# Small transformer: Silus of a result placed behind its last row, weighted sums of gathered rows with contiguous operands

## The chip, the cores and the metric

The kernel runs on one core of a Trainium2 chip. The metric is the device time of one execution in microseconds (us); three runs give its median. The profile is one further execution, whose own time is shown beside its span.

The engines are called as in the profile: PE (TensorE matmul; PEld is its weight load), DVE (VectorE), ACT (ScalarE), POOL (GpSimd) and SP (SyncE, which issues most transfers). PEclk is the TensorE clock that was granted, as a share of full speed.

## The reference

Four layers, each of them `x = x + attn(layernorm(x)) * silu(ffn(layernorm(x)))`, over 16 rows of 256 tokens with 128 features in float32. The change touches the end of layer 2 and layer 3.

Layer 2's feed-forward part is a mixture of 16 experts with two chosen for each token:

```python
topv, topi = jax.lax.top_k(probs, 2)
gate = jnp.sum(jax.nn.one_hot(topi, 16) * topv[..., None], axis=-2)
h = jax.nn.relu(jnp.einsum('bsd,edh->bseh', tensor, W1) + b1)
y = jnp.einsum('bseh,ehm->bsem', h, W2) + b2
out = jnp.einsum('bse,bsem->bsm', gate, y)
```

Layer 3 joins two parts that read the same normalized input:

```python
xn = _layernorm(x, axis=-1)
s = _L3_attn_ref(xn, ...)         # 16 heads of 8 features, with a penalty that depends on the distance
g = _silu(_L3_ffn_ref(xn, ...))   # two local transformer layers: attention in windows of 64, then a gated MLP
x = x + s * g
```

Each of the two local layers shifts half of the features by one token, projects to q, k and v with 8 heads of 64 features, attends within windows, adds the result to its input, and adds a gated MLP with an exact Gelu.

## The kernel before

Tokens lie on the 128 partitions, 32 tiles of 128 tokens. The arrays `x`, `xn`, `s` (the attention part) and `xnT` (the transposed input) stay in on-chip memory throughout.

**End of layer 2.** The experts wrote their results to DRAM, sorted by expert. For each tile `bring` (in `ffn2`) gathers the two chosen rows of each token with an indirect DMA from POOL's queue, and `weigh` adds both, times their gates, to the sum `f` (lines 1577 to 1582). `f` is a view of the memory of `xnT`, and the profile shows it under that name. The helper `mixed` (line 85) turns a row of 128 elements into a view of 64 x 2, so that elements are visited in the order 0, 64, 1, 65 and so on. Behind the sums, a Silu on ACT (line 937), a product with `s`, the sum into `x` and a layernorm give the input of layer 3. These pieces have names in the order list: `Ga` gathers a tile, `wa` weighs one, `su` is the Silu, `pw` the power of the layernorm.

**The local layers.** `local_layers` (called by `layer3`) works on blocks of 256 tokens; 16 blocks and two layers give 32 block numbers. Its work is cut into small pieces, one function each (decorator `@piece`). An order written out by hand, the string `LOCAL`, lists the pieces with a row number each; the loop "for turn in ..." runs through the list once for each turn, and a piece with row number r works on block turn + r. So a turn issues one block's worth of every piece, each at another stage of its block. ACT's pieces in a turn are copies of PSUM results (`hT`, `v`, `qT`, `kT`, `pT`, `oT`), squares (`sq`), 32 exponentials of the softmax (line 2033), and three Gelus (line 2177). Exponentials and Gelus need different function tables; a table load is an instruction of its own (ACT_TABLE_LOAD). The blocks' results are kept in place in `X`, which is the memory of `xn`; the last addition to a block is the piece `Z` (line 2205) of the second layer.

After the loop `pin(mark)` (line 988) binds every instruction since `mark` to the one ahead of it on the same engine, so that within the loop each engine issues in the order of the program text. Instructions outside of that are put in place by the framework's scheduler.

**The Silus.** Behind the call of `local_layers`, `layer3` issues eight Silus on ACT, each over four tiles of `X` (lines 1755 to 1757). They are outside of the pinned stretch, and the scheduler put seven of them between pieces of the second local layer, one in every second turn, and the eighth behind the last Gelu.

**The last attention.** `attn3` calls `attn8`. It projects q and k for two blocks at a time (`project`): a matmul into PSUM (line 292), an eviction with bias on ACT (line 299), a write to DRAM (`qkd`, line 301) and eight reads back in another layout (`qT`, `kT`, line 306), all on SP's queue. Then come the scores `pa` (line 345), their row maxima on DVE, the scores again, transposed (`pb`), the exponential, a product with the penalty, and the weighted values. The first two projections stand ahead of that function's own pinned loop. A later piece, `done`, multiplies `s` by `X` and adds it to `x`, and stores the result; it is the reader of the Silus.

Of the kernel before, what the change touches and what calls it, by code (L numbers as in the profile page):

```python
# [13 lines left out]
AF = mybir.ActivationFunctionType  # L14
ALU = mybir.AluOpType
# [8 lines left out]
NT = B * S // P  # L24
# [60 lines left out]
def mixed(*tiles):  # L85

    axes = {2: "p (a b) -> p b a", 3: "p t (a b) -> p t b a"}
    return [t.rearrange(axes[len(t.shape)], a=2) for t in tiles]


class Net:
# [20 lines left out]
    def load(self, pool, ap, name, shape=None, eng=None):  # L112
        t = pool.tile(list(shape or ap.shape), F32, name=name)
        (eng or self.nc.sync).dma_start(t, ap)
        return t
# [1201 lines left out]
    def ffn2(self, ctx, consts, f, keep):  # L1317
# [4 lines left out]
        nc, tc, a = self.nc, self.tc, self.a  # L1322
# [5 lines left out]
        wr, br, b1, step, row = consts  # L1328
        slot = keep.tile([P, K, NT], I32, name="slot", bufs=1)
        gate = keep.tile([P, K, NT], F32, name="gates", bufs=1)  # L1330
# [101 lines left out]
        placed, got = [], {}  # L1432
# [143 lines left out]

        def weigh(t):
            for k in range(K):
                y, row = mixed(f[:, t, :], got.pop(("rows", t, k)))
                nc.vector.scalar_tensor_tensor(  # L1580
                    y, row, gate[:, k, t : t + 1], y, ALU.mult, ALU.add
                )

        return {
            "send": send, "begin": begin, "piece": piece, "pieces": 4 * NB + 4, "bring": bring,
            "weigh": weigh, "spread": spread, "biases": biases, "biased": biased,
        }

# [149 lines left out]
    def layer3(self, end, out):  # L1738

        nc, tc = self.nc, self.tc
        X = self.xn
        right = lambda n, **kw: tc.tile_pool(name=n, bufs=1, side="right", **kw)
        with ExitStack() as ctx:
            gp = ctx.enter_context(right("a3_g"))
            dram = ctx.enter_context(tc.tile_pool(name="a3_d", bufs=1, space=DRAM))
            with right("f3_w") as cp:
                layers, load = self.local_weights(cp)
                with tc.tile_pool(name="l2_g", bufs=4) as got:  # L1750
                    gather = end["Ga"]
                    end["Ga"] = end["Gb"] = lambda: gather(got)
                    end["wb"] = end["wa"]
                    g, dr = self.local_layers(X, layers, load, end, lambda: self.gates3(gp, dram))
            for c in range(NT // 4):
                xc = X[:, 4 * c : 4 * c + 4, :]
                nc.scalar.activation(xc, xc, AF.Silu)

            def done(b, store):
                ts = slice(2 * b, 2 * b + 2)  # L1760
                if store:
                    nc.sync.dma_start(out[:, ts, :], self.x[:, ts, :])
                else:
                    attn, ffn = mixed(self.s[:, ts, :], X[:, ts, :])
                    nc.vector.tensor_mul(attn, attn, ffn)
                    nc.gpsimd.tensor_add(self.x[:, ts, :], self.x[:, ts, :], self.s[:, ts, :])

            self.attn3(g, dr, done)
# [83 lines left out]
        return r  # L1852

    def local_layers(self, X, layers, load, end, gates):

# [15 lines left out]
        nc, tc = self.nc, self.tc  # L1873
        with ExitStack() as ctx:
# [17 lines left out]
            rows = {b: {"l": layers[b // B], "X": X[:, 2 * (b % B) : 2 * (b % B) + 2, :]} for b in range(2 * B)}  # L1892
# [315 lines left out]
            gate, gates = gates()  # L2208
# [5 lines left out]
            for n in LOCAL.split():  # L2214
                n, row = n.split(":")
# [10 lines left out]
            for turn in range(-max(rows_), 2 * B - min(rows_)):  # L2226
                for n, args, row in order:
                    b = turn + row
                    if n in ("Ga", "Gb", "wa", "wb", "su", "pw"):
                        end[n]()  # L2230
                    elif n in ("gp", "ge", "gs", "gw", "gt", "gr"):
                        gate(n, b, psm)
                    elif 0 <= b < 2 * B:
                        do.get(n[0] + "_", do.get(n[0]))(b, *args)
                        w = spent.get(n + "".join(map(str, args)))
                        if b == B - 1 and w:
                            load(1, w)
            self.pin(mark)
            return gates

# [44 lines left out]
```

## Time and profile before

| | |
|---|---|
| median of 3 runs | 2729.04 us (2728.78 to 2735.28) |
| profiled execution | 2734.26 us, of which span 2732.5 us |
| mean granted TensorE clock | 0.918 |
| PE busy | 2346.4 us (86% of the span) |
| DVE busy | 1962.1 us (72%) |
| ACT busy | 1668.4 us (61%) |
| POOL busy | 1384.6 us (51%) |
| first and last weighted sum (line 1580, 64 of them) | 1435.8 and 1713.8 us |
| first and last table load for a Silu of line 1757 | 1994.7 and 2312.4 us |
| first score of the last attention (line 345) | 2322.4 us |

Times within the profile count from the start of the span. A line of the timeline gives start, duration, engine, line of the kernel, operation, output and inputs, and in brackets how long the engine had been idle and what ended that. A group's line gives busy time and mean duration, then the idle time ahead of the group. Instructions on ACT and DVE overlap by a little, so that the distance from start to start of two neighbours is up to 0.1 us shorter than the first one's duration. The busy share of an engine over the whole span says little about one stage, so stages are looked at in stretches of their own.

### The profile page before, as it was taken

How to read it: one execution, taken by the hardware profiler on the slowest of the kernel's cores; microseconds unless marked ns; L12 is line 12 of the kernel's file. 1: busy time of each engine (PE TensorE's matmuls, PEld its weight loads, DVE VectorE, ACT ScalarE, POOL GpSimd, SP SyncE). 2: the span in 40 equal slices, each digit the busy share in tenths (PEclk: the TensorE clock that was granted, in tenths of full speed). 3: DMA queues.
4: the chain of work that ended last, by engine and by line, in shares of the span. 5: the costliest groups of instructions: out<-in, count | busy, mean ns of one | idle time of the engine just before them, and what ended most of it. 6: DMA issues, size and time to landing. Idle time of an engine off the chain costs nothing.

```text
span 2732.5 us, 47736 instructions
## 1 busy us (share of the span) xinstructions
PE 2346.4 (86%) x17672; PEld 1560.2 (57%) x17735; DVE 1962.1 (72%) x3810; ACT 1668.4 (61%) x3680; POOL 1384.6 (51%) x1162
## 2 busy tenths in 40 slices
PE   6999997899756799999983789999999997889887
PEld 4666667566432455555561456666666665655554
DVE  6666633555579688888877899877776662788775
ACT  2555554233235466676641788888999896565653
POOL 3000001422417666666566667565654554798886
PEclk7999998899668899999996999999999998899987
DMA  3001002000114456556552000000000001121210
GB/s 84 24 29 33 17 17 101 6 11 12 35 54 152 142 165 196 180 182 189 173 185 57 21 22 23 15 19 18 24 11 11 13 14 32 33 46 30 49 30 9
DMA packets 136917, 168.25 MB, mean 62 GB/s; under 512 B 20850, under 2 KB 100604, under 8 KB 136684
## 3 DMA queue, kind: packets, MB, share of 16 engines
q1 hardware_dynamic: 128108, 147.09, 18.2%
q0 software_dynamic: 6496, 17.05, 1.8%
q8 instruction: 140, 2.29, 0.4%
q10 hardware_dynamic: 2080, 1.05, 0.1%
q14 instruction: 93, 0.76, 0.1%
HBM read 126.96 MB, written 29.79 MB: 57 GB/s over the span
## 4 chain that ended last, share of the span: by engine, by line
PE 27%; DVE 14%; ACT 11%; POOL 9%; issue 3%; DMA 2%; SPq 1%; POOLq 0%; DVEq 0%; ACTq 0%
PE py L1253 4%; ACT p L2033 3%; POOL e L333 3%; PE pm L2168 2%; PE pm L1922 2%; PE ps L2009 2%; PE ph L1496 2%; DVE pen L1715 2%; PE pa L1098 2%; PE pm L2096 1%; PE py L1519 1%; PE pb L355 1%; PE pa L345 1%; DVE sn L1948 1%; DVE ss L1944 1%
## 5 line engine op out<-in xcount | busy, mean ns | idle before, releaser
L366 DVE TENSOR_REDUCE nmax<-pa 128x2 f32<-128x512 f32 x512 | 329.6, 683 | 135.6 <-PE pb L355 109.1
L376 ACT ACTIVATE e<-pb 128x512 f32<-128x512 f32 x512 | 286.2, 594 | 226.8 <-PE pb L355 204.8
L355 PE MATMUL pb<-qa,kT 32*128 32x256 f32 x2048 | 388.4, 424 | 32.9 <-ACT e L376 32.9
L345 PE MATMUL pa<-kT,qT 32*128 32x256 f32 x2048 | 365.9, 435 | 10.9 <-DMA kT<-qkd 8.2
L1243 POOL TENSOR_TENSOR hc<-st,cn 128x1024 f32<-128x1024 f32 x111 | 261.2, 2353 | 193.7 <-DVE dbb L1226 120.9
L1230 DVE TENSOR_TENSOR_SCAN st<-dab,dbb 128x1024 f32<-128x1024 f32 x128 | 292.7, 2287 | 23.5 <-ACT dab L1216 8.1
L355 PEld LDWEIGHTS pb<-qa,kT 32*128 32x128 f32 x2048 | 249.8, 196 | 62.7 <-ACT e L376 54.0
L345 PEld LDWEIGHTS pa<-kT,qT 32*128 32x128 f32 x2048 | 231.4, 201 | 93.1 <-issue 56.2
L1253 PE MATMUL py<-hc,ident 128*128 128x512 f32 x512 | 270.6, 619 | 8.8 <-DVE hc L1243 7.4
L333 POOL TENSOR_TENSOR e<-e,pen 128x1024 f32<-128x1024 f32 x96 | 229.1, 2394 | 62.7 <-ACT e L376 61.5
L1922 PE MATMUL pm<-qkv,hT 128*128 128x512 f32 x384 | 211.9, 636 | 32.0 <-ACT p L2033 12.2
L2033 ACT ACTIVATE p<-ps,nm,rl 128x128 f32<-128x128 f32 x512 | 230.0, 474 | 12.2 <-DVE nm L2024 11.7
L1216 ACT ACTIVATE dab<-dl,A_log 128x512 f32<-128x512 f32 x256 | 177.7, 718 | 97.2 <-DVE st L1230 56.2
L178 POOL TENSOR_SCALAR ln_r<-ln_mv 128x4 f32<-128x4 f32 x32 | 8.5, 264 | 446.3 <-DVE ln_mv L189 438.6
L1957 POOL TENSOR_TENSOR rot<-rot,sn 128x512 f32<-128x512 f32 x128 | 162.6, 1274 | 125.7 <-DVE sn L1948 125.5
L1226 DVE TENSOR_TENSOR dbb<-du,bn 128x1024 f32<-128x1024 f32 x128 | 187.5, 1465 | 5.5 <-DMA bn<-dr 2.8
L2052 POOL TENSOR_TENSOR p<-p,den 128x512 f32<-128x512 f32 x128 | 130.5, 1041 | 39.7 <-DVE den L2047 30.7
L1253 PEld LDWEIGHTS py<-hc,ident 128*128 128x128 f32 x512 | 92.8, 197 | 80.7 <-issue 61.4
L1519 PEld LDWEIGHTS py<-w,h 128*128 128x128 f32 x752 | 101.1, 197 | 59.2 <-issue 39.7
L402 PE MATMUL pm<-e,vaug 128*32 128x256 f32 x2048 | 129.1, 394 | 3.6 <-DVE s L436 3.6
L1937 ACT ACTIVATE sq<-pm 128x512 f32<-128x512 f32 x128 | 76.4, 597 | 78.5 <-PE pm L1922 71.6
L1510 ACT ACTIVATE h<-ph,b1s 128x256 f32<-128x256 f32 x188 | 78.6, 470 | 70.0 <-PE ph L1496 69.1
(390 smaller groups left out, 5614.5 us busy)
## 6 DMA issues: line engine op xcount, KB each, us to landing
bn<-dr SPq DMA_DIRECT2D x64, 512.0 KB
cn<-dr SPq DMA_DIRECT2D x64, 512.0 KB
w<-in_L_ffn_W_dram SPq DMA_DIRECT2D x94, 256.0 KB
qkd<-qk SPq DMA_DIRECT2D x32, 256.0 KB
v<-v SPq DMA_DIRECT2D x64, 128.0 KB
f_y<-y SPq DMA_DIRECT2D x47, 128.0 KB
f_x<-zero POOLq DMA_DIRECT2D x8, 704.0 KB, 6.7
xr<-f_x SPq DMA_DIRECT2D x44, 128.0 KB
```

What stands on the lines that cost most here:

```text
L333: eng.tensor_mul(pairs[m], pairs[m], pen.to_broadcast([P, 2, 2, S]))
L345: nc.tensor.matmul(pa[:, t, :], qbuf[b % 4][r : r + 32, g, ts], kbuf[b % 4][r : r + 32, g, :], start=True, stop=True,)
L355: nc.tensor.matmul(pb[:, t, :], kbuf[b % 4][r : r + 32, g, ts], qas[m // 8][r : r + 32, g % 2, :], start=True, stop=True,)
L366: nc.vector.tensor_reduce(nbuf[n // 8 % 2][:, :, u // 4, u % 4, 8], pa, AX.X, ALU.max, negate=True)
L376: nc.scalar.activation(e, pb, AF.Exp, scale=scale)
L1216: nc.scalar.activation(d["da", r - r % 2][:, r % 2, :], d["dl"][:, h, :], AF.Exp, scale=an[:, h, n : n + 1])
L1226: mul = nc.vector.tensor_mul(db, du, d["bn", n])
L1230: nc.vector.tensor_tensor_scan(wide(d["st", r]), wide(d.pop(("da", r))), wide(db), 0.0, ALU.mult, ALU.add)
L1243: ins = eng.tensor_mul(d["hc", r], d.pop(("st", r)), d["cn", r // 4 * 2])
L1253: nc.tensor.matmul(d["py", h], self.ident, d["hc", r - r % 2][:, r % 2, :], start=(n == 0), stop=(n == N - 1))
L1922: nc.tensor.matmul(pj, hTs[b % 3][:, t * P : (t + 1) * P], rows[b]["l"]["qkv", j], start=True, stop=True,)
L2033: nc.scalar.activation(p[:, c, w, :], rows[b]["ps", u][i][:, c, w, :], AF.Exp, scale=rows[b]["r"][:, w, 0, h + 2 * c : h + 2 * c + 1], bia ...
```

## The change

Two edits. In `weigh`, the operands of the weighted sum are plain rows of 128 elements in place of the 64 x 2 views; operation, engine and number are the same. And the loop of eight Silus moves from `layer3` to the end of `local_layers`, between the loop over turns and `pin(mark)`, so that they are pinned on ACT behind the last piece.

```diff
@@ ffn2, weigh
             for k in range(K):
-                y, row = mixed(f[:, t, :], got.pop(("rows", t, k)))
                 nc.vector.scalar_tensor_tensor(
-                    y, row, gate[:, k, t : t + 1], y, ALU.mult, ALU.add
+                    f[:, t, :], got.pop(("rows", t, k)), gate[:, k, t : t + 1], f[:, t, :],
+                    ALU.mult, ALU.add,
                 )
@@ layer3
                     g, dr = self.local_layers(X, layers, load, end, lambda: self.gates3(gp, dram))
-            for c in range(NT // 4):
-                xc = X[:, 4 * c : 4 * c + 4, :]
-                nc.scalar.activation(xc, xc, AF.Silu)
-
             def done(b, store):
@@ local_layers, behind the loop over turns
                         if b == B - 1 and w:
                             load(1, w)
+            for c in range(NT // 4):
+                xc = X[:, 4 * c : 4 * c + 4, :]
+                nc.scalar.activation(xc, xc, AF.Silu)
             self.pin(mark)
             return gates
```

In the changed program's order of issue, ACT has eight Silus behind one table load after the last three Gelus and ahead of the eviction of the first q projection (in the kernel before: that eviction, a table load, one Silu, the eviction of k). SP issues both `qkd` writes, then the eight `qT` reads, then the eight `kT` reads; before, it issued the write and the reads of q, then the write and the reads of k. The order on PE, DVE and POOL is the same as before.

## The prediction

> **What bounds the kernel now.** The page's busy shares (PE 86%, DVE 72%, ACT 61%) average over stages with different limits, so I cut out the stages that the change touches: the windowed attention stage in front of layer 3 (1430 to 2314 us, one "turn" of the order list per 256 rows), and the seam behind it, where the last attention starts (2300 to 2325). First view: busy time in stretches, each from one Gelu table load on ACT to the next, so one turn each.
>
> ```profile
> core 0: us, PE busy (x) PEld busy (x) DVE busy (x) ACT busy (x) POOL busy (x), PEclk, DMA share, GB/s
> 1981.06:2006.11 25.05, 22.36 (x209) 15.47 (x210) 16.96 (x51) 24.05 (x63) 13.77 (x16) 1.00 0.05 12
> 2006.11:2029.28 23.17, 22.48 (x210) 15.83 (x211) 17.42 (x51) 21.19 (x60) 13.50 (x16) 1.00 0.06 13
> 2029.28:2055.10 25.82, 22.89 (x206) 15.82 (x206) 16.34 (x49) 24.33 (x63) 14.47 (x16) 0.93 0.05 11
> 2129.24:2155.33 26.09, 23.16 (x197) 16.26 (x201) 16.36 (x49) 24.33 (x63) 14.45 (x16) 0.89 0.05 12
> 2180.47:2205.64 25.17, 22.51 (x210) 15.74 (x211) 18.20 (x52) 24.05 (x62) 13.17 (x15) 1.00 0.05 13
> ```
>
> Columns: stretch and length, busy time by engine, granted TensorE clock. The turn without a Silu lasts 23.17 us with PE busy for 22.48 of it: PE sets its pace. Every second turn holds a Silu of line 1757; there ACT is busy for 24.1 to 24.3 us and the turn lasts 25 to 26: ACT sets its pace. Second view: ACT's timeline at the same place in a turn with and a turn without Silu.
>
> ```profile
> 1994.06 0.59 ACT L2068 COPY pT<-pt 128x512 f32<-128x512 f32 x1
> 1994.66 1.28 ACT L1757 ACT_TABLE_LOAD   x1
> 1995.96 0.63 ACT L1757 ACTIVATE xn<-xn 128x512 f32<-128x512 f32 x1
> 1996.49 0.58 ACT L1937 ACTIVATE sq<-pm 128x512 f32<-128x512 f32 x1
> 1997.34 1.28 ACT L2033 ACT_TABLE_LOAD   x1
> 1998.64 0.46 ACT L2033 ACTIVATE p<-ps,nm,rl 128x128 f32<-128x128 f32 x1
> ...
> 2019.40 0.59 ACT L2068 COPY pT<-pt 128x512 f32<-128x512 f32 x1
> 2020.89 0.60 ACT L1937 ACTIVATE sq<-pm 128x512 f32<-128x512 f32 x1 [0.89 <-PE pm L1922]
> 2021.81 0.46 ACT L2033 ACTIVATE p<-ps,nm,rl 128x128 f32<-128x128 f32 x1
> ```
>
> With the Silu, the exponentials begin 4.58 us after the copy of pT; without it, 2.41, of which 0.89 is waiting for PE. The chain of waits confirms it: both table loads of Silus 1 to 5 stand on it.
>
> **Part 1, the Silus leave the turns.** Of the eight 128x512 Silus, seven sat inside turns. In the changed program's order of issue they and 13 table loads are gone from there (two loads each for the first six; one for the seventh, behind which a Gelu load comes anyway); all other orders inside the turns are as before. From ACT alone, one such group is 1.28 + 0.53 (start to start) + 1.28 = 3.1 us; but 0.89 us of waiting for PE comes back, so about 2.2 is won. The turns themselves say it more surely. Gelu to Gelu, pairs of turns (one with, one without a Silu) took 48.22, 49.94, 50.02, 51.23 and 48.35 us for Silus 1 to 5; two plain turns are 2 x 23.17 = 46.34. Excess: 1.88, 3.60, 3.68, 4.89, 2.01, sum 16.1 us. (The two plain turns ahead of Silu 1, 1934.49 to 1981.06, average 23.29, by which it were 14.9; a little of layer 1's extra work is in them, so I keep 16.1.)
>
> Two things are in it. The pairs of Silus 1 and 5, at a clock of 1.00 in both turns, show the bare stall: 1.95 us, times five 9.7. The other 6.4 us go with a lowered clock: 2050.86 to 2054.27, 2102.06 to 2105.47 and 2149.85 to 2156.67 stand at 0.50, each 6.7 to 8.9 us behind the Silu's table load, and from 1529 to 2050 the clock stood at 1.00 throughout. Behind the Silu at 2043 PE stood still for 0.78 (DVE sn) and 1.72 us (ACT qT), and was busy for 1.77 of the 4.26 us up to 2050.86; the drop follows. [...] I take the rows, since drops occur in this stretch only behind Silus, and keep 9.7 as the upper end of the time.
>
> Silu 6 (2242.09) lies in the ramp-down. Its own load isn't on the chain, but the exponentials' reload at 2244.69 is (1.28), and the 0.50 stretch 2248.83 to 2255.66 slows the eight L2168 matmuls from 1.92 to 3.26 us and L2009 from 1.03 to 1.99 (2.3 together). That may recur without the Silu, as PE thins out there; half of it gives 1.2, so -2.5 (ends -1.3 and -3.6). Silu 7 (2286.25): the second pT copy behind it waits 0.48 for PE anyway: 0 (end -1.9).
>
> **Part 2, the Silus at the seam.** They now stand behind the last Gelu (ends 2311.0) and ahead of the query projection's eviction; the changed SP order sends both qkd writes first, then the eight qT reads, then the eight kT reads.
>
> ```profile
> 2312.40 0.33 SPq L301 DMA_DIRECT2D qkd<-qk  x1
> 2314.47 2.72 SPq L306 DMA_DIRECT2D qT<-qkd  x8
> 2317.29 0.34 SPq L301 DMA_DIRECT2D qkd<-qk  x1
> 2320.17 2.69 SPq L306 DMA_DIRECT2D kT<-qkd  x8
> 2322.35 8.48 PE L345 MATMUL pa<-kT,qT 32*128 32x256 f32 x40 [8.24 <-DMA kT<-qkd]
> ```
>
> Before: q's write at 2312.40, its reads 2.07 later, and k's write stuck in SP's queue behind them until 2317.29 although its eviction ended at 2314.90. After, on the same clock: table load 2311.0 to 2312.3, Silus 0.53 apart, so the eighth starts at 2316.0 (its row is added by DVE at 2313.33, so it doesn't wait), q's eviction at 2316.5 to 2317.2, k's to 2317.8. q's write 2317.25, reads 2319.3 to 2322.0; k's write 2317.8 lands by 2320.7 (2.88 as before), its reads go out from 2322.1, PE starts 2.18 later: 2324.3. So +2.0 us. Queued behind the Silus on ACT are the penalty's pieces (u, lo, hi), which waited for POOL's lo until 2317.7 anyway. PE's v projection needs the q eviction for its PSUM buffer and starts some 4 us later, at 2317.3, still ahead of the scores. Ends: 0 and, if SP's new order recovered nothing, +4.9.
>
> **Part 3, the weighted sums (64 on DVE).**
>
> ```profile
> L1580 DVE SCALAR_TENSOR_TENSOR xnT<-got,gates,xnT x64: 409/446/4110, 1435.8 to 1713.8; 128x128 f32<-128x128 f32 x64
> L830 DVE SCALAR_TENSOR_TENSOR y<-py,f_oh,y 128x128 f32<-128x128 f32 x256 | 72.1, 344 | 64.7 <-PE py L826 60.2 <-issue 2.5 <-ACT qf L634 1.8
> ```
>
> The first line (the view of one source line) gives min/median/max ns: 446 with interleaved operands. The nearest contiguous row is line 830: same operation, size and per-row scalar, 344; it reads one operand from PSUM. A contiguous one with both in SBUF is line 1341, 128x512 in 686; less 384 elements at 1.05 ns it is 282, without a scalar from memory. I take 344: -0.10 each (end -0.16). The 22 sums up to 1469 mostly wait for the gather (18.3 us of idle DVE); the other 42 form 21 pairs in the turns, where DVE is busy for 23.7 of 24.8 us and the sums are on the chain (7.8% of it). In a pair the first takes 0.44, the second 1.25 to 1.5: it waits until a POOL operation has ended (at 1600.13 it starts beside rot at 1600.14 and ends 0.23 after it). [...] From the row alone, 64 x (0.773 mean - 0.344) = 27 would seem to be at stake. I take -3. Ends: at seven pairs of the 1.5 kind DVE loses by 10 ns; if it now comes first, -7 more, with POOL 0.3 later; if the first sums come to wait too, +17 and more.
>
> **Sum.** -16.1 - 2.5 - 0 + 2.0 - 3.0 = -19.6 us. The profiled run took 2734.26 (span 2732.5 and 1.8 around it), so 2714.7 on its footing; it lies 5.2 above the median of the timed runs, 2729.04, so 2709 against that. The last attention (407 us) is moved and not changed: its blocks run at 23.8 us on average while one low-clock stretch falls on two blocks, at 24.5 in the last five, where they are denser; all blocks in the one or the other mode give -4 to +7, kept for the range.
>
> **Rivals.**
> A, the sum above: 2709; chance 0.45.
> B, the clock: the drops have another cause, or the median run has fewer than the profiled one (it is 5.2 shorter). Then 6.4 of part 1 is missing: 2716; 0.18. [...] Against: the order in time.
> C, DVE comes first at the lock in the seven pairs: 2702; 0.17. For it: the 10 ns. Against: POOL's copy ahead of rot is itself released sooner when the first sum ends sooner.
> D, the change does little: bare stall only, the seam at +4.9, the dense mode in all blocks of the last attention: -9.7 - 1.3 + 4.9 - 2 + 7 = -1, so 2728; with less of each, down to some 2714; 0.12 in all. For it: all these costs are in the trace. Against: no one thing makes them come together.
> E, slower: the contiguous sum meets POOL's lock also in the first of each pair. It needs 20 + 8 = 28 us, or 1.3 us for each of the 21 pairs; a wait of the usual 0.8 gives +17 and a time of 2726, one of two POOL p products (2.04) on top of each first sum gives +43, so 2752. For it: one sum at 1501.11 took 4.11. Against: POOL's rot comes 0.15 us after the first sum, and the 0.1 gained doesn't change that. 0.08.
>
> About 0.3% (8 us) is what a measurement can tell from no change. Below 2720.9 lie A, C, nearly all of B and half of D: 0.85 faster; the rest of B and D and the cheaper part of E are within the bound, 0.09; slower is E beyond it, 0.06. The range reaches from C with the sparser mode of the last attention (2696) to the near part of D (2722).
>
> **What would show it.** Turns of 23.2 us in pairs from 1960 to 2230 with ACT busy near 21 us and the clock at 1.00; eight Silus in a row with one load; the first scores about 2 us later behind the last Gelu; sums at 0.34 us, seconds of pairs still above 1. It is wrong if the drops stay, if pairs remain above 47 us because something else paces the plain turn too, or if pairs of sums grow.

## The result, and the profile after

The changed kernel takes 2718.53 us, median of seven runs (2714.97 to 2722.88); the kernel before, run beside it, takes 2734.58 us (seven runs, 2728.78 to 2740.57). The ratio is 0.9943, with a 95% interval of 0.9925 to 0.9961: faster by 0.57%, or 15.6 us, where the forecast said 19.6. The profiled execution spans 2716.7 us (before 2732.5), with the same mean granted clock of 0.918.

First the turns, in the same view and columns as in the prediction: busy time in stretches from one Gelu table load on ACT to the next. One that held Silu 2:

```profile
2025.65:2048.81 23.16, 22.63 (x212) 15.84 (x211) 17.41 (x51) 21.16 (x60) 13.88 (x16) 1.00 0.06 13
```

Every turn is now a plain one: most last 23.16 us, with PE busy for 22.63 of it and ACT for 21.2, and the last ones, at the end of this stage, 23.5 to 23.9; all of them run at full clock (PEclk 1.00). On ACT's timeline the exponentials of L2030 (formerly L2033) begin 2.40 us after the copy of pT, in a turn that had a Silu, and the wait for PE is back:

```profile
1992.63 0.59 ACT L2065 COPY pT<-pt 128x512 f32<-128x512 f32 x1
1994.11 0.60 ACT L1934 ACTIVATE sq<-pm 128x512 f32<-128x512 f32 x1 [0.89 <-PE pm L1919]
...
1995.03 0.46 ACT L2030 ACTIVATE p<-ps,nm,rl 128x128 f32<-128x128 f32 x1
```

At the seam (timeline, all engines) the eight Silus stand in one row behind one load, and the first score comes 15.10 us after the start of the last Gelu (2294.07), where it was 11.74. In the lines of SP (SPq, its queue), a duration is the time that issuing took:

```profile
2294.07 0.47 ACT L2174 ACTIVATE mu<-pm,b 85x256 f32<-85x256 f32 x1 [1.05 <-PE pm L2165]
2294.56 1.28 ACT L2237 ACT_TABLE_LOAD   x1
2295.85 4.26 ACT L2237 ACTIVATE xn<-xn 128x512 f32<-128x512 f32 x8
2300.02 0.67 ACT L299 ACTIVATE qk<-pm,qadd 128x512 f32<-128x512 f32 x1
2300.71 0.90 SPq L301 DMA_DIRECT2D qkd<-qk  x2
2302.79 2.71 SPq L306 DMA_DIRECT2D qT<-qkd  x8
2305.60 3.34 SPq L306 DMA_DIRECT2D kT<-qkd  x8
2309.17 8.35 PE L345 MATMUL pa<-kT,qT 32*128 32x256 f32 x40 [7.21 <-DMA kT<-qkd]
```

**Where the time went.** To set traces side by side I cut each at the same events. The names in the table, with the times of the kernel before: *ahead*, up to the first weighted sum (1435.84); *sums*, from there to the Gelu load at 1981.06, with all 64 sums and a stretch without change behind them; *Silus 1-5*, the ten turns to the load at 2228.82; *Silu 6*, two turns to 2273.54; *ramp-down*, to the start of the last Gelu at 2310.61; *seam*, to the first score at 2322.35; *last*, the last attention, to the end of the span. The first row gives lengths in us, the others the difference to it, each from one profiled execution. The kernels e1 to e8 are the experiments of the next section.

| kernel | ahead | sums | Silus 1-5 | Silu 6 | ramp-down | seam | last | span |
|---|---|---|---|---|---|---|---|---|
| before | 1435.84 | 545.22 | 247.76 | 44.72 | 37.07 | 11.74 | 410.12 | 2732.5 |
| **changed** | +0.8 | -2.2 | -15.4 | -2.2 | +2.5 | +3.4 | -2.6 | 2716.7 |
| e1 sums only | -1.3 | -2.8 | -2.8 | -2.3 | +1.3 | +0.2 | -2.4 | 2722.4 |
| e2 Silus only | +8.1 | +1.2 | -15.3 | -3.6 | -1.0 | +3.4 | +5.9 | 2731.2 |
| e3 no Silu | +2.9 | -2.9 | -15.4 | -3.7 | -1.5 | -0.9 | -2.6 | 2708.4 |
| e4 late Silus | -1.5 | -1.4 | -15.4 | -3.7 | -1.5 | -0.7 | -2.6 | 2705.7 |
| e5 copies | +2.8 | -0.4 | -15.3 | -3.6 | +3.0 | -0.5 | +4.4 | 2722.9 |
| e6 filled | +8.9 | +0.6 | -5.6 | -0.9 | +1.5 | +0.6 | -2.4 | 2735.2 |
| e7 changed again | +3.0 | -1.3 | -15.3 | -3.6 | +2.1 | +3.4 | -0.1 | 2720.6 |
| e8 late again | -0.6 | -1.6 | -15.4 | -3.7 | +2.1 | -0.8 | -2.5 | 2709.9 |

The first column shows how little a single span says: up to 1435.84 all these kernels issue the same work, and still they lie 10 us apart. The columns from the sums to the seam are steadier (all but the ramp-down, which is taken up below), and the experiments are read from them.

### The profile page after: what moved, and what is told of

It reads as the page before. It is cut to its first block, busy times and chain, and to the rows that moved or that the text cites. A ratio compares the mean times of both kernels' runs of the same rounds, so it can differ in the third digit from the quotient of the medians.

```text
span 2716.7 us, 47773 instructions
## 1 busy us (share of the span) xinstructions
PE 2347.6 (86%) x17735; PEld 1556.3 (57%) x17735; DVE 1959.7 (72%) x3810; ACT 1649.8 (61%) x3667; POOL 1385.2 (51%) x1162
## 4 chain that ended last, share of the span: by engine, by line
PE 30%; DVE 13%; POOL 8%; ACT 8%; issue 3%; DMA 3%; SPq 1%; POOLq 0%; DVEq 0%; ACTq 0%
PE py L1253 4%; PE pm L1919 3%; POOL e L333 2%; PE pm L2165 2%; PE ps L2006 2%; PE ph L1496 2%; ACT p L2030 2%; PE pm L2093 2%; DVE pen L1715 2%; PE po L2075 2%; PE pa L1098 2%; PE py L1519 2%; PE pb L355 1%; PE pm L1982 1%; PE pa L345 1%
## 5 line engine op out<-in xcount | busy, mean ns | idle before, releaser
L2030 ACT ACTIVATE p<-ps,nm,rl 128x128 f32<-128x128 f32 x512 | 229.8, 474 | 10.6 <-DVE nm L2021 10.0
```

Of the source, the lines that this page charges most:

```text
L2030: nc.scalar.activation(p[:, c, w, :], rows[b]["ps", u][i][:, c, w, :], AF.Exp, scale=rows[b]["r"][:, w, 0, h + 2 * c : h + 2 * c + 1], bia ...
```

## The experiments

**The two edits apart.** e1 is the kernel before with the contiguous sums alone; e2 is the changed kernel with the sums taken back.

```diff
@@ e1: weigh, in the kernel before
-                y, row = mixed(f[:, t, :], got.pop(("rows", t, k)))
                 nc.vector.scalar_tensor_tensor(
-                    y, row, gate[:, k, t : t + 1], y, ALU.mult, ALU.add
+                    f[:, t, :], got.pop(("rows", t, k)), gate[:, k, t : t + 1], f[:, t, :],
+                    ALU.mult, ALU.add,
                 )
@@ e2: the same lines, in the changed kernel, the other way round
```

In the prediction and in the next text "lock" is a name for a wait that the traces show, and for no more: of the 21 second sums of pairs in the kernel before, 19 overlap with a POOL operation, end 0.2 to 0.3 us behind its end and take 1.06 to 2.08 us, where the first sums of their pairs take 0.43 to 0.45.

> Only the sums' operands are made contiguous; the Silus stay in the turns. From the trace of the changed kernel: between 1435 and 1740 us it gains 2.2 us, and the seven sums that lost POOL's lock now take 0.35 us, with the wait of about 1 us handed to the next DVE instruction (line 946 or 958). If the sums are worth what that stage shows: about -2 us against the kernel before (within the noise of a time, but visible as -2.2 in the trace at 1740, and unchanged from there to 1980). Rival (the price of the lock is won): -7 or more.

> Only the Silus are moved; the sums stay interleaved. Main theory: about -13.5 us against the kernel before (-16.1 for Silus 1 to 5, -2 to -4 in the ramp-down, +3.4 at the seam, +2 to +4 at the end of the ramp-down if its clock drops fall as in the changed kernel). Trace: plain turns of 23.2 us throughout the second local layer and no clock drop between 1560 and 2230 us. Rival (the sums matter more): -10 or less.

e1 ran at 0.9986 of the kernel before (0.9976 to 0.9996; 20 runs against 23), some 3.8 us less; e2 at 0.9949 (0.9932 to 0.9966), some 13.9 less. Both together make 17.7, and the whole change had 15.6: the edits add up within their intervals, and about four fifths of the gain are the Silus'. The stages agree. With contiguous sums (changed, e1, e3, e4, e7, e8) the stage of the sums is 1.3 to 2.9 us shorter than before; without them (before, e2, e5, e6) it is between 0.4 shorter and 1.2 longer. Means -2.0 and +0.3, so about 2.4 us for the 64 sums. The profiled span of e2 is nearly that of the kernel before, but only because of what lies outside of the change: 8 us ahead of it and 6 in the last attention. (e1's -2.8 in the column of Silus 1 to 5 is not the edit's: two half-clock stretches lie there in its trace, three in that of the kernel before.)

What the sums gave, and what took it, is in the groups of DVE instructions from 1475 to 1714 us (count | busy us, mean ns | idle before). The kernel before:

```profile
L1580 DVE SCALAR_TENSOR_TENSOR xnT<-got,gates,xnT 128x128 f32<-128x128 f32 x41 | 39.3, 959 | 0.7
L958 DVE TENSOR_TENSOR gate<-gate,s 128x512 f32<-128x512 f32 x5 | 6.3, 1251 | 0.0
L946 DVE TENSOR_SCALAR xn<-x,ln_mv,ln_r 128x128 f32<-128x128 f32 x20 | 5.7, 387 | 0.0
```

The changed kernel:

```profile
L1579 DVE SCALAR_TENSOR_TENSOR xnT<-got,gates,xnT 128x128 f32<-128x128 f32 x41 | 28.4, 693 | 0.7
L946 DVE TENSOR_SCALAR xn<-x,ln_mv,ln_r 128x128 f32<-128x128 f32 x20 | 10.1, 607 | 0.0
L958 DVE TENSOR_TENSOR gate<-gate,s 128x512 f32<-128x512 f32 x5 | 9.5, 1898 | 0.0
```

The sums lost 10.9 us and the two instructions that follow some of them took 4.4 and 3.2 more: 7.6 of the 10.9 were handed on. Of the 3.3 that stayed, 2.1 are the 21 first sums of the pairs, 0.1 each. One place of it, from DVE's and POOL's timelines of the kernel before:

```profile
1573.77 1.98 DVE L1580 SCALAR_TENSOR_TENSOR xnT<-got,gates,xnT 128x128 f32<-128x128 f32 x2
1574.25 1.26 POOL L1957 TENSOR_TENSOR rot<-rot,sn 128x512 f32<-128x512 f32 x1
1575.60 1.09 DVE L958 TENSOR_TENSOR gate<-gate,s 128x512 f32<-128x512 f32 x1
```

and of the changed kernel:

```profile
1573.52 0.73 DVE L1579 SCALAR_TENSOR_TENSOR xnT<-got,gates,xnT 128x128 f32<-128x128 f32 x2
1573.98 1.39 POOL L1954 TENSOR_TENSOR rot<-rot,sn 128x512 f32<-128x512 f32 x1
1574.16 2.17 DVE L958 TENSOR_TENSOR gate<-gate,s 128x512 f32<-128x512 f32 x1
```

The second sum now starts 0.08 us ahead of POOL's rot and takes 0.35 us (both in 0.73); before, the second took 1.50 by itself and ended 0.24 behind rot. But rot is still running when L958 starts, and now L958 takes 2.17 in place of 1.09 us.

**The load or the activation.** e5 is the kernel before with a copy in place of each Silu: the same eight activations of the same size, put in place by the scheduler as before, but without a table of their own, so that 14 loads of 1.28 us disappear: the eight ahead of the Silus and six that brought the exponentials' table back. e3 is the changed kernel without any Silu at all.

```diff
@@ e5: layer3, in the kernel before
             for c in range(NT // 4):
                 xc = X[:, 4 * c : 4 * c + 4, :]
-                nc.scalar.activation(xc, xc, AF.Silu)
+                nc.scalar.activation(xc, xc, AF.Identity)
@@ e3: end of local_layers, in the changed kernel
-            for c in range(NT // 4):
-                xc = X[:, 4 * c : 4 * c + 4, :]
-                nc.scalar.activation(xc, xc, AF.Silu)
```

> The kernel before with its eight Silus turned into plain copies in place (Identity), at the same places; the Silu itself is left out, so the last product takes the feed-forward part without it. An Identity needs no table load, so 14 loads go and eight ACT instructions of 0.6 us stay. If the loads are what stalls the turns: the copy fits into the 0.89 us for which ACT waits for PE, two turns take 46.3 to 46.5 us, no clock drop lies between 1990 and 2230 us, and the trace gains about 15 us there, like the kernels without Silus in the turns. Rival (it is the activations themselves, or the order): pairs of turns stay at 47.5 us or above and drops remain.

> The changed kernel with the eight Silus left out altogether (so the last product takes the feed-forward part without its Silu). Price of the Silus where they stand now: main theory, the q and k evictions come 5.5 us sooner, of which SP's order and the reads' time give back a part: first score 3.4 to 4.7 us sooner behind the last Gelu, and the time 3 to 5 us under the changed kernel's. Rival (the seam is hidden behind POOL's preparations): below 1 us.

e5: 0.9942 (0.9924 to 0.996; 10 runs against 27). The turns of Silus 1 to 5 are 15.3 us shorter, as if the activations had gone; they are still there, with ACT busy for 21.7 of 23.2 us in such a turn. So the whole cost inside the turns was that of the loads, with what hangs on them. e3: 0.9947 (0.993 to 0.9963; 4 runs against 23). The 3 to 5 us under the changed kernel that were expected do not show in the time (the changed kernel had 0.9943 in a comparison of its own). They show in the trace: e3's seam lies 4.3 us below that of the changed kernel, which is what the Silus and their load cost there.

**The clock.** The prediction split the 16.1 us of the turns into 9.7 of bare stall and 6.4 of lowered clock, and rival B left the second part out. e6 keeps the kernel before, Silus, loads and all, and only fills PE's gap behind the load with three more matmuls, which repeat the product of the v projection just made.

```diff
@@ e6: local_layers, the v projection, behind its matmul
+                if t == 0 and b - 1 in (20, 22, 24, 26, 28, 30):
+                    for _ in range(3):
+                        nc.tensor.matmul(
+                            rows[b]["pj", t, 2][:, 0:256],
+                            hTs[b % 3][:, t * P : (t + 1) * P],
+                            rows[b]["l"]["qkv", 2][:, 0:256],
+                            start=True,
+                            stop=True,
+                        )
```

> The kernel before, with three more matmuls (256 columns, 1.55 us together, the same product again into the same place) in the six turns with a Silu, at the point where PE stood still for 1.72 us waiting for ACT's qT copy. Loads and Silus stay. If low PE activity behind the Silu is what halves the clock: no drop between 1990 and 2230 us, pairs of turns of 48.2 us each, about 6 us less than the profiled kernel before in that stretch. [...]

PE's timeline of the kernel before, behind the Silu at 2043, just ahead of the stretch at half clock (2050.86 to 2054.27):

```profile
2047.73 1.10 PE L1922 MATMUL pm<-qkv,hT 128*128 128x512 f32 x2 [0.78 <-DVE sn L1948]
2050.54 0.85 PE L1985 MATMUL pm<-ident,rot 128*128 128x128 f32 x4 [1.72 <-ACT qT L1992]
```

The same place in e6, where the second gap is 0.42 in place of 1.72 us:

```profile
2058.17 1.46 PE L1935 MATMUL pm<-qkv,hT 128*128 128x256 f32 x6
2060.05 0.66 PE L1994 MATMUL pm<-ident,rot 128*128 128x128 f32 x4 [0.42 <-ACT qT L2001]
```

and e6's turn with that Silu as a stretch, columns as above:

```profile
2038.79:2064.15 25.36, 24.00 (x218) 16.98 (x217) 17.22 (x51) 24.24 (x63) 14.28 (x16) 1.00 0.05 12
```

The turns with a Silu are still ACT's (24.2 us busy, 25.36 long, against 23.18 for the plain turn behind the first of them), but none of them falls to the half clock any more. The ten turns take 242.13 us: 5.6 less than before with more work on PE, and 9.8 more than in the changed kernel. So in the profiled execution of the kernel before the bare stall is 9.8 (predicted 9.7) and the clock's share is 5.6 (predicted 6.4). The share is one execution's: in e1, with two half-clock stretches, it is 2.9. In time e6 ran at 0.9968 (0.9953 to 0.9983; 10 runs against 27), faster than before by adding matmuls. Between 1990 and 2230 the half clock is found behind three of the five Silus in the kernel before and behind two in e1, the two kernels that have loads and gaps; in the other eight, with no loads or with the gap filled, it is found nowhere in that stretch. Since it came behind five Silus of ten where nothing was filled, none in five for e6 would be 1 in 32 by chance.

The record of the granted clock in the traces says more than this chance. In each of the ten traces every change of the clock falls on one grid of 3.413 us (within 0.003 us), and that grid lies differently against the program in each trace. So PE's busy time can be cut along the grid. (Where a matmul ends is modelled in the profile, so such a share is an estimate.) Two such windows of the kernel before, in the gaps behind Silus 1 and 2:

```profile
1999.66:2003.07 3.41, 1.69 (x18) 0.89 (x16) 1.95 (x4) 3.41 (x13) 1.59 (x3) 1.00 0.03 7
2047.45:2050.86 3.41, 1.42 (x5) 0.62 (x6) 2.00 (x6) 3.41 (x14) 2.33 (x3) 1.00 0.00 0
```

PE is busy for 50% of the first, and the clock stays up; for 42% of the second, and the half clock begins where it ends. All windows at full clock between 1540 and 2320 us, from all ten traces:

| PE busy in the window | windows | followed by half clock |
|---|---|---|
| under 44% | 27 | 27 |
| 44 to 56% | 37 | 15 |
| over 56% | 2123 | 0 |

Behind each of the ten unfilled Silus lies one window with 34 to 54%: those with 34, 42, 46, 50 and 50% were followed by the half clock, those with 50, 50, 52, 52 and 54% were not. The two gaps are 0.6 to 0.8 and 1.7 us behind all ten; how much of them falls into one window is a matter of where the grid lies. In e6 no window of these turns is under 71%.

**The Silus behind the seam.** e4 takes the eight Silus one step further: tied on ACT behind the evictions of the first two projections and the first pieces of the penalty, ahead of the first exponential of the last attention, where ACT waits for the scores.

```diff
@@ e4: local_layers, in the changed kernel
-            for c in range(NT // 4):
-                xc = X[:, 4 * c : 4 * c + 4, :]
-                nc.scalar.activation(xc, xc, AF.Silu)
@@ layer3
+            def first():
+                ins = list(nc.cur_bb.bb.instructions)
+                silus = [
+                    nc.scalar.activation(X[:, 4 * c : 4 * c + 4, :], X[:, 4 * c : 4 * c + 4, :], AF.Silu)
+                    for c in range(NT // 4)
+                ]
...
@@ attn8, behind the first projections and the first penalty
+            if first is not None:
+                first()
```

> The changed kernel with the eight Silus behind the first two projections' evictions and the first penalty, ahead of the first exponential's table load, where ACT is idle for some 12 us. Main theory: as without the Silus, 3 to 5 us under the changed kernel, so about -19 to -20 against the kernel before. Rival (ACT's later start of the second penalty or the table load delays the first exponential): no gain over the changed kernel.

Its timeline at the seam:

```profile
2298.20 8.35 PE L345 MATMUL pa<-kT,qT 32*128 32x256 f32 x40 [7.51 <-DVE pen L1717]
2300.95 4.26 ACT L1770 ACTIVATE xn<-xn 128x512 f32<-128x512 f32 x8
```

The Silus run while PE makes scores; from the last Gelu to the first score it is 11.01 us, 4.1 less than in the changed kernel, and the last attention takes no longer for it (-2.6 in both). So the trace wins 4.1 us at this stage. The time: 0.9933 (0.9912 to 0.9954; 4 runs against 23), some 18.3 us less than before, which does not stand clear of the changed kernel's 15.6.

**Both again, side by side.** Whether e4 is the better kernel and whether the loss in the ramp-down recurs was asked of a second run of the changed kernel (e7) and of e4 (e8), beside each other, without a further edit.

> The changed kernel once more, for a direct comparison with the late Silus: about -15 us against the kernel before. The seam (last Gelu to first score) again near 15.1 us; the end of the ramp-down is expected to be 4 to 5 us shorter than in the first trace of this kernel, where a 10 us clock drop lay in it.

> The kernel with the Silus behind the first penalty once more, beside the changed kernel: seam of 11.0 us, so 4 us under the changed kernel and about -19 us against the kernel before. Rival: no difference to the changed kernel in time, as the later blocks of the last attention take the gain back.

e7: 0.9939 (0.992 to 0.9959; 9 runs), e8: 0.9932 (0.9909 to 0.9956; 7 runs). In the trace e8 has the same 4.2 us less at the seam, so that is shown twice; in time the two can't be told apart: 4 us is 0.15%, and the runs of one kernel spread over 8 to 21 us. By its trace e4 is the kernel to keep; no interval here shows it faster than the changed one.

For the ramp-down the expectation of e7 failed: it was to be 4 to 5 us shorter, and the loss came again (+2.1), also in e8, whose first run did not have it. PE's instructions there, and their order, are the same in all of them. From the view in stretches, a piece of the changed kernel's ramp-down:

```profile
2266.40:2276.60 10.20, 8.89 (x43) 6.62 (x44) 2.03 (x4) 4.81 (x9) 2.21 (x4) 0.50 0.00 0
```

and PE's timeline at its beginning:

```profile
2265.63 0.67 PE L2075 MATMUL po<-pT,v 128*64 128x128 f32 x12 [1.12 <-ACT pT L2065]
2267.05 1.97 PE L2058 MATMUL pt<-ident,p 128*128 128x128 f32 x8 [0.75 <-POOL p L2049]
```

The same work in e4, as a stretch:

```profile
2264.90:2279.60 14.70, 9.99 (x80) 8.23 (x80) 4.08 (x11) 5.02 (x10) 2.83 (x7) 1.00 0.10 15
```

and on PE's timeline:

```profile
2263.66 0.67 PE L2092 MATMUL po<-pT,v 128*64 128x128 f32 x12 [1.12 <-ACT pT L2082]
2265.08 1.09 PE L2075 MATMUL pt<-ident,p 128*128 128x128 f32 x8 [0.75 <-POOL p L2066]
```

Same gaps of 1.12 and 0.75 us, and then 10.2 us at half clock in one (the eight matmuls of pt take 1.97 us) and none in the other (1.09). The changed kernel, e5, e7 and e8 have these 10.2 us, and their ramp-downs are 2.1 to 3.0 longer than before; e2, e3 and e4 don't, and theirs are 1.0 to 1.5 shorter. The order of PE's instructions does not tell these seven traces apart; where the grid of 3.413 us lies does: in the four traces with the loss a window ends 0.2 to 0.8 us behind the start of the first matmul shown (po), in the three without it 2.5 us behind it. PE is busy for 49 to 52% of that window in all seven, so the share alone does not tell them apart.

## Why the prediction was right, and where it was not

The forecast for the profiled footing was -19.6; the span shows -15.8. In time, 2709 was forecast against a kernel before at 2729.04; the changed kernel took 2718.53, inside the range of 2696 to 2722, beside a kernel before at 2734.58. By the number alone it lies nearest to rival B's 2716; which mechanism it was is seen only in the steps:

| step | predicted | measured | |
|---|---|---|---|
| part 1, Silus 1 to 5 | -16.1 | -15.4 | split 9.7 + 6.4, found 9.8 + 5.6 |
| part 1, Silu 6 | -2.5 | -2.2 | |
| part 1, Silu 7 and the ramp-down | 0 | +2.5 | a half-clock stretch of 10.2 us not in the sum |
| part 2, seam | +2.0 | +3.4 | reads of kT |
| part 3, sums | -3.0 | -2.2 | rival C's event came, most of its gain was handed on |
| ahead and last attention | 0 | -1.8 | +0.8 and -2.6, no part of the change; luck |

**Silus 1 to 5.** The reading by turns held, and so did the choice to count the lowered clock with the bare stall: e6 leaves the Silus, brings the longest gap from 1.72 us to 0.42, and the clock's share goes. PE was never idle for a whole window behind a Silu: windows with PE busy for 34 to 50% were followed by the half clock. The first half of rival B, that the drops have another cause and stay, is refuted for these turns. Its second half, that other executions have fewer drops than the profiled one, stays possible: e1's had two.

The 9.8 beside the predicted 9.7 is in part luck. The prediction took 1.95 us for each of five Silus; against the changed kernel the pairs of e6 are longer by 2.2 us for each of the first four, which is what it had worked out from ACT alone, and by 1.0 for the fifth. Its yardstick of two plain turns, 46.34, held for the first four pairs (46.02, 46.32, 46.33 and 46.33 in the changed kernel) and not for the last, where the plain turns themselves take 47.35; why they lengthen there was not looked into. The missing 0.7 us of the step are there.

**Silu 6, Silu 7, ramp-down.** Silu 6 came out at -2.2 with a half-clock stretch (2232, 3.4 us) still in it, and at -3.6 in six other executions that have no Silu load there, which is the other end that the prediction gave: "half of it" was the right kind of value. The zero for Silu 7 was too cautious where the clock stays up (-1.0 to -1.5 in e2, e3 and e4; its end was -1.9). What the sum lacked is the clock behind it: the prediction counted half-clock stretches as something that the change takes away and allowed for none that could newly come in the ramp-down. It cost this execution about 4 us (+2.5 against -1.5 in e3 and e4).

**The seam.** Counted from the start of the last Gelu, the steps came as worked out: q's write 6.64 us behind it (6.64 predicted), the reads of qT at 8.72 (8.7), those of kT at 11.53 (11.5). The term that was mis-sized is the last: "PE starts 2.18 later" was taken from reads of kT that had the queue to themselves. Now they go out right behind the eight reads of qT; the eight issues take 3.34 in place of 2.69 us, and the first score comes 3.57 behind the first issue. All seven traces with this order show 3.6 to 4.0, the three with the old one (before, e1, e6) 2.2 to 2.4. Four of the seven (e3, e4, e5, e8) have no Silu ahead of these reads, so it is not the Silus that lengthen them; that it is the eight reads ahead in the queue is argued from the order, since no run changed that alone.

**The sums.** The rate (0.446 to 0.351, predicted 0.344) held. The -3.0 was my estimate, and no run shows it as a term of its own; what they show is 2.2 us less in this stage, or 2.4 by the means of the ten traces, with 2.1 less in the 21 first sums. Most of the waits for POOL stayed with contiguous operands: 12 of the 19 second sums that waited still take 1.06 to 1.25 us. At the seven others, of the kind that DVE had lost by 10 ns, it now comes first, which was rival C's event. Its -7 did not come, since the instruction behind the pair meets the same POOL operation and takes longer in its place (L958 2.17 in place of 1.09 us, L946 1.35 in place of 0.38); that step is in neither the sum nor the rivals. Rival E, first sums that come to wait, did not happen: 20 of the 21 take 0.32 to 0.35 us, and the one long one (4.02) was there before (4.11).

Rival D's dear seam came in part (+3.4, between the +2.0 of the sum and the +4.9 of the rival), without D's other costs. One sum of the prediction is off by a little: C with the sparser mode of the last attention is 2702 - 4 = 2698, not 2696.

## What to carry to other kernels

Where a paced loop holds an activation with a function table of its own, look at the loads first: here the price was that of two loads of 1.28 us and not of the activation (plain copies in its place made the ten turns 15.3 us shorter, no activation there 15.4), and, where PE waited for that engine, also 3.4 to 6.8 us at half clock behind three of five Silus. Gather such activations behind one load, and put them where that engine waits anyway (here behind the first projections rather than ahead of them: 11.01 us in place of 15.10 from the last Gelu to the first score, by the trace). Before counting a wait for another engine as won, look at which instruction runs next while that engine's operation is still going: here 7.6 of the 10.9 us were handed on. Do not carry over a latency from a transfer that had its queue free: right behind eight other reads, the first score came 3.57 us behind the first issue of kT's, where 2.18 had been counted.

## What the runs showed of the hardware that I had not expected

- The half clock came here without a long gap, at 2050.86 in the kernel before behind gaps of 0.78 and 1.72 us; with the second filled down to 0.42 us it came at none of five places of one execution (e6). In the ten traces its stretches begin and end on a grid of 3.413 us, and it goes with PE's share of the window of that grid just ahead: at under 44% it came in 27 windows of 27, between 44 and 56% in 15 of 37, above that in none of 2123 (1540 to 2320 us).
- So one program lost some us in one execution and kept them in another: gaps of 1.12 and 0.45 to 0.76 us in the ramp-down brought 10.2 us of half clock in four traces and none in three, and of two executions of one kernel e8 had them and e4 did not.
- Also a DVE instruction with one tensor operand and two scalars per row (L946) took longer beside POOL: the first of a group of four behind a pair of sums takes 1.35 us beside rot in place of 0.38, the other three 0.39 each. The group took 1.15 us at that place before the change (at 1601.49) and takes 2.13 now (at 1599.85).
- POOL pays too, but little: rot takes 1.39 us at the six places where a second sum now comes first, and 1.26 to 1.32 elsewhere.
- The last attention, which no edit here touches but for its first 5 us, took 410.12 us before and 407.5 to 416.1 in the other traces: -2.6 to -2.4 in six of them, about 0 in one, +4.4 and +5.9 in two, by no rule of the edits. It and the part ahead of the sums set how small a difference can still be told.
